# Attention's gathering of v: v as the stationary operand, both halves of a block in two column tiles, turned back per block

## The chip, the core and the metric

The kernel runs on one core of a Trainium2 chip. The metric is the device time of one execution, in microseconds (us); lower is better. The chip's engines run side by side, each with its own instruction stream in a fixed order: TensorE (PE, with its weight loads shown apart as PEld), VectorE (DVE), ScalarE (ACT), GpSimd (POOL) and SyncE (SP), which issues the transfers.

## What is computed

The program applies four layers to x, of shape 32 x 192 x 56 x 56 in float32, each as x + layer(group norm of x). The change is in layer 0, an attention through 49 "agent" tokens in six heads. Its reference, cut to what matters:

```python
qkv = xf @ Wqkv + bqkv
q, k, v = (qkv[..., :c], qkv[..., c:2 * c], qkv[..., 2 * c:])
agent = qi.mean(axis=(2, 4)).reshape(b, A, c)
...
agent_attn = softmax(einsum('bhad,bhnd->bhan', ah * scale, kh) + pos_bias, axis=-1)
agent_v = einsum('bhan,bhnd->bhad', agent_attn, vh)
...
q_attn = softmax(einsum('bhnd,bhad->bhna', qh * scale, ah) + agent_bias, axis=-1)
out = einsum('bhna,bhad->bhnd', q_attn, agent_v)
...
out = out + dw.transpose(0, 2, 3, 1).reshape(b, n, c)
out = out @ proj_w + proj_b
```

`agent_v` is the product in question: for each head the 49 agents' weights over all 3136 pixels, times v. `dw` is a 3 x 3 depthwise convolution of v.

## The kernel before

Attention is the function `attention` (from L321). It runs over NB = 32 images, called batches here. An image is cut into NK = 4 blocks of columns, three of 16 and one of 8 columns (WIDTHS), and each block into an upper and a lower half of 28 rows: 448 (or 224) pixels per half. A half is further cut into pieces of SUB = 112 pixels, `ns` = 4 (or 2) per half. The six heads are taken as three pairs; one pair has PAIR = 98 agents, and HA = 294 is all of them.

For each block j a first loop does, in this order of the program:

- `weigh` (L592): for each head pair the scores of 98 agents over the block's pixels, on PE (L600, L601); their maximum on DVE (L602, `low`); the exponential on ACT (L604), which leaves `pr` and its sums.
- `seen` for q in block 0, and from block 1 on `gather` of the block before (L633).
- `turn` (L610): the transposes of v (L619, copied by ACT into `vT`, L620) and of `pr` (L627, copied by ACT into `prT`, L630).
- `find_v` (L553) of block j + 2: v on PE, copied by ACT into the padded images `v_a`, `v_c` (L561, L569) and into `v`.
- `convolve` (L575) of block j + 1: eight taps each for two channel groups on DVE (L587). A block's taps read one column of the next block, so they wait for its `find_v`. In the last block `moments` of the next image (L450) takes that place.

`gather` multiplies, for each head pair, `prT` (112 pixels x 98 agents, stationary) by `vT` (112 pixels x 64 channels, streaming) and sums over all pieces of both halves in PSUM; the result has the agents on its partitions, and DVE copies it to `got[:, j]` (L642).

After the loop come `ask(0)` (L666: scores of the pixels over the agents on PE, L674 and L675, their softmax on DVE and ACT, L678 to L691), the last block's `gather`, and `join` (L644), which scales the four blocks' `got` to a common maximum on DVE (L647 to L662) and leaves `values`. A second loop over t then runs `ask(t)`, `turn_back` (L694, transposes L701), `project` (L722) and `answer` (L709, which multiplies `values` by the turned weights, L714 and L719), with the next image's normalisation, agents and first two `find_v` between.

PSUM has four buffers of two banks for all of this (tag "ps"), each given to the next user once its readers are done. A planner orders the instructions on each engine when the program is built; the order is then fixed. On DVE and ACT it differs from the program's in places, for instance one `vT` copy stands before the third exponential. An instruction that waits holds up all that follows on its engine.

Of the kernel before, what the change touches and what calls it, by code (L numbers as in the profile page):

```python
# [20 lines left out]
F32 = mybir.dt.float32  # L21
I32 = mybir.dt.int32
AF = mybir.ActivationFunctionType
ALU = mybir.AluOpType
# [4 lines left out]
C = 192  # L29
# [14 lines left out]
PAIR = 2 * AG  # L44
HA = HEADS * AG
# [275 lines left out]
def attention(ctx: ExitStack, tc: tile.TileContext, a, k, x1):  # L321
# [6 lines left out]
    nc = tc.nc  # L328
# [3 lines left out]
    wp = ctx.enter_context(tc.tile_pool(name="a_w", bufs=2))  # L332
    sp = ctx.enter_context(tc.tile_pool(name="a_s", bufs=2))
    pp = ctx.enter_context(tc.tile_pool(name="a_p", bufs=4, space=PSUM))
    mm = nc.tensor.matmul
    UP, LOW = slice(0, 64), slice(64, 128)
    HALVES = ((0, UP), (1, LOW))
    P2 = slice(0, PAIR)

    def psum():  # L340
        return pp.tile([128, 2, BANK], F32, name="ps", tag="ps")
# [85 lines left out]
    def small(name, shape):  # L427
        return sp.tile(shape, F32, name=name, tag=name)
# [21 lines left out]
    def moments(x):  # L450

        st_a, st_c = small("st_a", [128, 7, 6]), small("st_c", [128, 4, 6])
        flat = [t.rearrange("p y x -> p (y x)") for t in x]
        for i in range(7):
            nc.vector.bn_stats(st_a[:, i], flat[0][:, i * 448 : (i + 1) * 448])
        for i in range(4):
            nc.vector.bn_stats(st_c[:, i], flat[1][:, i * 392 : (i + 1) * 392])
        mv = small("mv", [128, 2, 2])
        nc.vector.bn_aggr(mv[:, 0], st_a.rearrange("p a b -> p (a b)"))
        nc.vector.bn_aggr(mv[:, 1], st_c.rearrange("p a b -> p (a b)"))  # L460
        pool_a, pool_c = small("pool_a", [128, AG]), small("pool_c", [65, AG])
        by_x = [wp.tile([128, n, POOL], F32, name="by_x", tag=f"by_x{n}", bufs=1) for n in (S, S // 2)]
        for t in range(2):
            nc.vector.tensor_reduce(
                by_x[t].rearrange("p y q -> p (y q)"), x[t].rearrange("p y (q x) -> p (y q) x", x=8), AX.X, ALU.add
            )
        nc.vector.tensor_reduce(
            pool_a.rearrange("p (w q) -> p w q", w=POOL), by_x[0].rearrange("p (w y) q -> p w q y", y=8), AX.X, ALU.add
        )
        fours = small("fours", [64, 2 * POOL, POOL])  # L470
        for h, r in HALVES:
            nc.vector.tensor_reduce(
                fours[:, h * POOL : (h + 1) * POOL], by_x[1][r].rearrange("p (w y) q -> p w q y", y=4), AX.X, ALU.add
            )
        nc.vector.tensor_tensor(
            pool_c[0:64].rearrange("p (w q) -> p w q", w=POOL), fours[:, 0::2], fours[:, 1::2], ALU.add
        )
        nc.vector.memset(pool_c[64:65], 1.0)
        return mv, (pool_a, pool_c)
# [130 lines left out]
    def turn(j, prs, v):  # L610

        _, _, ns = sizes(j)
        vT = wp.tile([SUB, 4, 3 * 128], F32, name="vT", tag="vT")
        for s0 in range(0, ns, 2):
            ps = psum()
            for i in range(2):
                px = slice((s0 + i) * SUB, (s0 + i + 1) * SUB)
                for c in range(3):
                    nc.tensor.transpose(ps[:SUB, i, c * 128 : (c + 1) * 128], v[:, c, px], ident)  # L619
            nc.scalar.copy(vT[:, s0 : s0 + 2], ps[:SUB, :, : 3 * 128])  # L620
        prT = wp.tile([SUB, 8, HA], F32, name="prT", tag="turned", bufs=2)
        for q in range(0, 2 * ns, 2):
            ps = psum()
            for i in range(2):
                h, s = divmod(q + i, ns)
                for p in range(3):
                    nc.tensor.transpose(  # L627
                        ps[:SUB, i, p * PAIR : (p + 1) * PAIR], prs[p][:, h, s * SUB : (s + 1) * SUB], ident[P2, P2]
                    )
            nc.scalar.copy(prT[:, q : q + 2], ps[:SUB, :, :HA])  # L630
        return prT, vT

    def gather(j, prT, vT, got):  # L633
        _, _, ns = sizes(j)
        ps = psum()
        for p in range(3):
            out = ps[P2, 0, p * 64 : (p + 1) * 64]
            for q in range(2 * ns):
                h, s = divmod(q, ns)
                c = h * 128 + p * 64 if p < 2 else 256 + h * 64  # L640
                mm(out, prT[:, q, p * PAIR : (p + 1) * PAIR], vT[:, s, c : c + 64], start=(q == 0), stop=(q == 2 * ns - 1))
        nc.vector.tensor_copy(got[:, j], ps[P2, 0, :C])  # L642

    def join(low, sums, got):  # L644

# [20 lines left out]
    def ask(j, g):  # L666
        _, _, ns = sizes(j)
        pq = wp.tile([SUB, 8, HA], F32, name="pq", tag="turned", bufs=2)
        for q0 in range(0, 2 * ns, 4):
            for q in range(q0, q0 + 4, 2):  # L670
                ps = psum()
                for i in range(2):
                    px = slice((q + i) * SUB, (q + i + 1) * SUB)
                    mm(ps[:SUB, i, :HA], xs_a[j][:, px], g, start=True, stop=False)  # L674
                    mm(ps[:SUB, i, :HA], xs_c[j][0:KC, px], gq_c[0:KC, 2 * j + (q + i) // ns], start=False, stop=True)  # L675
                by_head = ps[:SUB, :, :HA].rearrange("p i (h g) -> p i h g", g=AG)
                mx = sp.tile([SUB, 2, HEADS], F32, name="mx", tag="mx", bufs=4)
                nc.vector.tensor_reduce(mx, by_head, AX.X, ALU.max)  # L678
                nc.vector.tensor_tensor(
                    pq[:, q : q + 2].rearrange("p i (h g) -> p i h g", g=AG),  # L680
                    by_head,
                    _bc(mx, [SUB, 2, HEADS, AG]),
                    ALU.subtract,
                )
            flat = pq[:, q0 : q0 + 4].rearrange("p i c -> p (i c)")
            rows = flat.rearrange("p (r g) -> p r g", g=AG)
            nc.scalar.activation(flat, flat, AF.Exp)
            sm = sp.tile([SUB, 4 * HEADS], F32, name="sm", tag="sm", bufs=4)
            nc.vector.tensor_reduce(sm, rows, AX.X, ALU.add)
            nc.vector.reciprocal(sm, sm)  # L690
            nc.vector.tensor_tensor(rows, rows, _bc(sm, [SUB, 4 * HEADS, AG]), ALU.mult)  # L691
        return pq
# [53 lines left out]
    for b in range(NB):  # L746
        x, more = nxt, b + 1 < NB
        if more:
            nxt = load(b + 1)
        low, sums, got = small("low", [PAIR, NK, 3]), small("sums", [PAIR, NK, 3]), small("got", [PAIR, NK, C])  # L750
        turned, asked, back = {}, {}, {}
        for j in range(NK):
            prs = weigh(j, gk, low, sums)
            if j == 0:
                gq = seen(ag, wqT, gq_c, "gq_a")
            else:
                gather(j - 1, *turned[j - 1], got)
            turned[j] = turn(j, prs, v[j])
            if j + 2 < NK:
                v[j + 2] = find_v(j + 2)  # L760
            if j + 1 < NK:
                o[j + 1] = convolve(j + 1)
            elif more:
                mv, pools = moments(nxt)
        asked[0] = ask(0, gq)
        gather(NK - 1, *turned[NK - 1], got)
        values = join(low, sums, got)
        done, o = o, {}
        for t in range(1, NK + 2):
            if t < NK:  # L770
                asked[t] = ask(t, gq)
            if more and t == 1:
                mean, d = spread_of(mv)
            if t <= NK:
                back[t - 1] = turn_back(t - 1, asked[t - 1])
            if more and t in (3, 4):
                v[t - 3] = find_v(t - 3)
            if t >= 2:
                project(t - 2, done[t - 2], x)
            if t <= NK:  # L780
                answer(t - 1, back[t - 1], values, done[t - 1])
            if more and t == 1:
                rs, nb = scaling(mean, d, pools)
                normed(nxt, rs, nb, 0)
            if more and t == 2:
                ag = find_agents(b + 1, pools)
                normed(nxt, rs, nb, 1)
            if more and t == 3:
                gk = seen(ag, wkT, gk_c, "gk_a")
                normed(nxt, rs, nb, 2)  # L790
            if more and t == 4:
                o[0] = convolve(0)
                normed(nxt, rs, nb, 3)
        nc.sync.dma_start(out=x1[b, 0:128], in_=x[0].rearrange("p y x -> p (y x)"))
        for h, r in HALVES:
            nc.sync.dma_start(out=x1[b, 128:C, 1568 * h : 1568 * h + 1568], in_=x[1][r].rearrange("p y x -> p (y x)"))
# [909 lines left out]
```

## Time and profile before

| what | value |
|---|---|
| median of 3 runs | 14596.81 us (14577.73 to 14602.56) |
| profiled execution, its own time | 14588.21 us |
| profiled execution, span of its instructions | 14586.4 us |
| granted TensorE clock, mean | 0.927 |
| busy: PE, PEld, DVE, ACT, POOL | 84%, 52%, 78%, 41%, 15% |
| attention loop | about 330 to 5320 us |
| in it busy: PE, DVE, ACT | 4662, 4022 and 2369 of 4990 us |
| gather's matmuls (L641) | 5376 matmul records (as many weight loads), median 250 ns (167 ns) |
| gather's copy (L642) | 128 on DVE, median 356 ns |

Busy time is the time in which an engine has an instruction in flight, as a share of the span. Matmuls are pipelined and overlap each other in the records, so the spacing of their starts says more than the length of one. A float32 matmul of the program shows as two records of PE and two weight loads, a transpose as one. Idle time stands before the instruction that ended it, with the engine and line that released it. "granted clock" is the share of full speed that TensorE's clock was given.

### The profile page before, as it was taken

To read this page: it belongs to the slowest core of one execution; us is meant where nothing else is said; L and a number is where in the kernel's file an instruction comes from. 1 tells how busy PE (TensorE), PEld (TensorE's weight loads), DVE (VectorE), ACT (ScalarE), POOL (GpSimd) and SP (SyncE) were. 2 spreads that over 40 slices of the span, in tenths; PEclk is the share of its full clock that TensorE was granted. 3 is DMA by queue.
4 is the path that set the end of the run, shared out by engine and by line. 5 is a ranking of instruction groups with operands and counts; after the bars stand their busy time and mean duration, and the time that the engine had idled before them with its cause. 6 is when DMAs were issued, how large, how long until landed. Compare 5 with 4: busy or idle time off the path is not lost. (4 is left out here: it accounts for less than half of the span.)

```text
span 14586.4 us, 164705 instructions
## 1 busy us (share of the span) xinstructions
PE 12276.2 (84%) x63542; PEld 7620.1 (52%) x63542; DVE 11320.3 (78%) x15929; ACT 5972.2 (41%) x10826; POOL 2178.7 (15%) x2238
## 2 busy tenths in 40 slices
PE   4999999999999976777677677767899889988898
PEld 2655655655565553333333333335666666666666
DVE  4878877887887878878887887886777777777777
ACT  2444444444444434444444444443323232323323
POOL 0000000000000004434443443442000000000000
PEclk8999999999999988888888888888999999999999
DMA  2001001000100112232223222322111111111111
GB/s 54 27 27 40 27 27 40 27 27 32 35 27 27 40 53 66 60 71 71 65 67 81 66 60 68 75 51 56 35 37 36 37 37 36 37 35 38 36 37 23
DMA packets 886784, 654.14 MB, mean 45 GB/s; under 512 B 764942, under 2 KB 772857, under 8 KB 876976
## 3 DMA queue, kind: packets, MB, share of 16 engines
q1 hardware_dynamic: 885992, 643.51, 16.7%
q8 instruction: 505, 8.27, 0.2%
q14 instruction: 287, 2.35, 0.1%
HBM read 402.88 MB, written 240.50 MB: 44 GB/s over the span
## 5 line engine op out<-in xcount | busy, mean ns | idle before, releaser
L587 DVE SCALAR_TENSOR_TENSOR o<-v_a,dww,o 128x896 f32<-128x896 f32 (+1 forms) x1024 | 1052.8, 1028 | 390.1 <-ACT v_a L561 282.7
L1633 ACT COPY y<-ps 64x252 f32<-64x252 f32 (+1 forms) x2376 | 807.6, 340 | 1298.6 <-PE ps L1627 1266.4
L1567 PE MATMUL ps<-f,imag 84*84 84x112 f32 x6144 | 1032.0, 261 | 130.2 <-DVE imag L1560 128.5
L1574 ACT COPY z<-ps 84x448 f32<-84x448 f32 x768 | 405.3, 528 | 1771.1 <-PE ps L1567 1771.1
L1567 PE MATMUL ps<-f,real 84*84 84x112 f32 x6144 | 1035.7, 261 | 1.7
L1567 PEld LDWEIGHTS ps<-f,imag 84*84 84x84 f32 x6144 | 744.0, 153 | 275.6 <-DVE imag L1560 206.4
L1567 PEld LDWEIGHTS ps<-f,real 84*84 84x84 f32 x6144 | 748.8, 153 | 160.1 <-issue 68.6
L1041 ACT ACTIVATE q<-q 128x784 f32<-128x784 f32 x384 | 329.3, 858 | 1225.4 <-DVE q L1036 1223.9
L1035 POOL COPY c<-p 128x1 f32<-128x1 f32 x384 | 696.2, 1813 | 665.3 <-DVE p L1034 611.8
L1048 POOL MEMSET c<- 128x1 f32 x192 | 18.3, 99 | 5182.8 <-PE ps L719 5172.1
L1034 DVE TENSOR_TENSOR_SCAN q<-decay,c,ek 128x784 f32<-128x784 f32 x384 | 702.0, 1832 | 105.3 <-ACT ek L1064 105.2
L1583 PE MATMUL ps<-z,f 84*114 84x448 f32 x1536 | 658.5, 551 | 129.5 <-ACT z L1574 129.5
L604 ACT ACTIVATE pr<-ps,low 98x896 f32<-98x896 f32 (+1 forms) x384 | 350.1, 914 | 1015.4 <-DVE low L602 1015.4
L1585 DVE TENSOR_TENSOR o<-ps,rs 114x448 f32<-114x448 f32 x384 | 239.5, 624 | 631.7 <-PE ps L1583 630.5
L1035 POOL COPY c<-q 128x1 f32<-128x1 f32 x384 | 483.1, 1258 | 1460.7 <-DVE q L1034 1390.3
L1034 DVE TENSOR_TENSOR_SCAN p<-decay,c,bv 128x784 f32<-128x784 f32 x384 | 699.9, 1833 | 0.0
L674 PE MATMUL ps<-gq_a,xs_a 128*112 128x294 f32 x1792 | 643.7, 442 | 0.0
L600 PE MATMUL ps<-xs_a,gk_a 128*98 128x448 f32 (+1 forms) x1536 | 639.0, 497 | 0.0
L587 DVE SCALAR_TENSOR_TENSOR o<-v_c,dww,o 128x448 f32<-128x448 f32 (+1 forms) x1024 | 634.0, 619 | 4.0
L1547 PE MATMUL re<-y,f 128*84 128x420 f32 (+1 forms) x1152 | 561.5, 569 | 84.8 <-ACT y L1633 74.8
L601 PE MATMUL ps<-xs_c,gk_c 125*98 125x448 f32 (+1 forms) x1536 | 631.6, 492 | 0.0
L675 PE MATMUL ps<-gq_c,xs_c 125*112 125x294 f32 x1792 | 627.7, 433 | 0.0
(352 smaller groups left out, 29243.6 us busy)
## 6 DMA issues: line engine op xcount, KB each, us to landing
x<-x SPq DMA_DIRECT2D x512, 392.0 KB
x<-x SPq DMA_DIRECT2D x512, 196.0 KB
x<-x SPq DMA_DIRECT2D x192, 399.0 KB
out_x<-x SPq DMA_DIRECT2D x384, 196.0 KB
x_a<-in_x SPq DMA_DIRECT2D x32, 1568.0 KB
x<-x_a SPq DMA_DIRECT2D x32, 1568.0 KB
x_c<-in_x SPq DMA_DIRECT2D x64, 392.0 KB
x<-x_c SPq DMA_DIRECT2D x64, 392.0 KB
```

The costliest lines, as they stand in the source:

```text
L587: nc.vector.scalar_tensor_tensor(dst, tap(i), dww[:, t, i : i + 1], dst, ALU.mult, ALU.add)
L600: mm(ps[P2, h, :n], g[:, cols], xs_a[j][:, px], start=True, stop=False)
L601: mm(ps[P2, h, :n], gk_c[0:KC, 2 * j + h, cols], xs_c[j][0:KC, px], start=False, stop=True)
L674: mm(ps[:SUB, i, :HA], xs_a[j][:, px], g, start=True, stop=False)
L675: mm(ps[:SUB, i, :HA], xs_c[j][0:KC, px], gq_c[0:KC, 2 * j + (q + i) // ns], start=False, stop=True)
L1034: nc.vector.tensor_tensor_scan(out, decay[:, of(t)].to_broadcast([128, MC]), data, at, ALU.mult, ALU.add)
L1035: nc.gpsimd.tensor_copy(at, s[:, last : last + 1])
L1547: nc.tensor.matmul(ps[:, : n * 84], f2[:, i, :], y[:, i0 : i0 + n].rearrange("p g s u -> p (g s u)"), start=True, stop=True)
L1567: nc.tensor.matmul(ps[:84, i * 2 * S : (i + 1) * 2 * S], part[:, i0 + i].rearrange("p s u -> p (s u)"), f3[:, m, :], start=(m == 0), stop= ...
L1574: nc.scalar.copy(z[:, i0 : i0 + n].rearrange("p g m w -> p (g m w)"), ps[:84, : n * 2 * S])
L1583: nc.tensor.matmul(got, f4[:, m, :], z[:, i0 : i0 + n, m, :], start=(m == 0), stop=(m == 1))
L1633: nc.scalar.copy(y[64 * m : 64 * m + 64, 2 * g0 + i : 2 * (g0 + n) : 2], got[64 * i : 64 * i + 64, :, :, m, :])
```

## The change

`gather` exchanges the operands: `vT` (64 channels of one half) is stationary, `prT` (98 agents) streams. The upper half's products go to PSUM partitions 0 to 63 and the lower half's to 64 to 127, so that neighbouring matmuls of the two halves lie in two column tiles of the array. The sum then has channels on the partitions and the halves apart. ACT copies it to a new tile `halves`. A new function `settle` turns it back with three transposes, after which ACT copies one half to `got` and DVE adds the other. `settle` stands behind `turn` of the following block. The last block's `gather` moves from behind `ask(0)` to in front of it, and its `settle` stands behind `ask(0)`. `got` has one buffer instead of two.

```diff
-    def gather(j, prT, vT, got):
+    def gather(j, prT, vT):
+
         _, _, ns = sizes(j)
         ps = psum()
         for p in range(3):
-            out = ps[P2, 0, p * 64 : (p + 1) * 64]
-            for q in range(2 * ns):
-                h, s = divmod(q, ns)
-                c = h * 128 + p * 64 if p < 2 else 256 + h * 64
-                mm(out, prT[:, q, p * PAIR : (p + 1) * PAIR], vT[:, s, c : c + 64], start=(q == 0), stop=(q == 2 * ns - 1))
-        nc.vector.tensor_copy(got[:, j], ps[P2, 0, :C])
+            cols = slice(p * PAIR, (p + 1) * PAIR)
+            for s in range(ns):
+                for h, r in HALVES:
+                    c = h * 128 + p * 64 if p < 2 else 256 + h * 64
+                    mm(ps[r, 0, cols], vT[:, s, c : c + 64], prT[:, h * ns + s, cols], start=(s == 0), stop=(s == ns - 1))
+        halves = wp.tile([128, HA], F32, name="halves", tag="halves")
+        nc.scalar.copy(halves, ps[:, 0, :HA])
+        return halves
+
+    def settle(j, halves, got):
+
+        ps = psum()
+        for p in range(3):
+            nc.tensor.transpose(ps[P2, 0, p * 128 : (p + 1) * 128], halves[:, p * PAIR : (p + 1) * PAIR], ident)
+        both = ps[P2, 0, : 3 * 128].rearrange("p (a h d) -> p a h d", a=3, h=2)
+        nc.scalar.copy(got[:, j].rearrange("p (a d) -> p a d", a=3), both[:, :, 0])
+        mine = got[:, j].rearrange("p (a d) -> p a d", a=3)
+        nc.vector.tensor_tensor(mine, mine, both[:, :, 1], ALU.add)
...
-        low, sums, got = small("low", [PAIR, NK, 3]), small("sums", [PAIR, NK, 3]), small("got", [PAIR, NK, C])
+        low, sums = small("low", [PAIR, NK, 3]), small("sums", [PAIR, NK, 3])
+        got = sp.tile([PAIR, NK, C], F32, name="got", tag="got", bufs=1)
         turned, asked, back = {}, {}, {}
         for j in range(NK):
             prs = weigh(j, gk, low, sums)
             if j == 0:
                 gq = seen(ag, wqT, gq_c, "gq_a")
             else:
-                gather(j - 1, *turned[j - 1], got)
+                halves = gather(j - 1, *turned[j - 1])
             turned[j] = turn(j, prs, v[j])
+            if j > 0:
+                settle(j - 1, halves, got)
             if j + 2 < NK:
                 v[j + 2] = find_v(j + 2)
...
+        halves = gather(NK - 1, *turned[NK - 1])
         asked[0] = ask(0, gq)
-        gather(NK - 1, *turned[NK - 1], got)
+        settle(NK - 1, halves, got)
         values = join(low, sums, got)
```

## The prediction

> **What bounds the kernel now.** The change touches the attention stage alone, so I first look for that stage and for its limit. The page's busy shares in 40 slices (one slice is 365 us) show it: PE at nine tenths from slice 2 on, DVE at seven or eight.
>
> ```profile
> PE   4999999999999976777677677767899889988898
> ...
> DVE  4878877887887878878887887886777777777777
> ...
> PEclk8999999999999988888888888888999999999999
> ```
>
> The whole attention loop runs from about 330 to 5320 us, 32 batches of 158.7 us (by the starts of gq_a's copy, L533: 157.7 and 159.7 in turn). Read as one stage it says "PE". I cut one batch into three stretches (busy us and counts of PE, PEld, DVE, ACT, POOL, then granted clock):
>
> ```profile
> 2052.60:2122.00 69.40, 66.35 (x408) 44.77 (x406) 59.33 (x85) 33.78 (x62) 0.00 (x0) 1.00 0.22 70
> 2122.00:2150.00 28.00, 25.01 (x134) 17.58 (x132) 27.16 (x45) 8.53 (x10) 0.00 (x0) 0.96 0.00 1
> ```
>
> Where three of the four gathers stand (first row) PE is busy 66.4 of 69.4 us. Where ask, join and the first answer stand (second row) DVE is: 27.2 of 28.0. So time saved on PE ahead of that stretch counts only if DVE's chain moves too. Next, the timeline of PE, ACT and DVE around the first gather (start, us, what, idle before):
>
> ```profile
> 2082.81 4.29 PE L641 MATMUL ps<-vT,prT 112*98 112x64 f32 x48
> 2086.94 1.48 PE L619 MATMUL ps<-ident,v 128*112 128x128 f32 x12
> 2088.25 0.78 PE L627 MATMUL ps<-ident,pr 98*112 98x98 f32 x4
> 2089.65 1.90 PE L627 MATMUL ps<-ident,pr 98*112 98x98 f32 x20 [0.62 <-ACT pr L604]
> 2091.38 0.57 PE L559 MATMUL ps<-xs_a,wv_a 128*128 128x224 f32 x2
> ```
> ```profile
> 2087.80 0.80 ACT L620 COPY vT<-ps 112x768 f32<-112x768 f32 x1 [0.96 <-PE ps L619]
> 2088.49 1.01 ACT L604 ACTIVATE pr<-ps,low 98x896 f32<-98x896 f32 x1
> ```
> ```profile
> 2084.62 2.08 DVE L602 TENSOR_REDUCE low<-ps 98x1 f32<-98x896 f32 x2
> 2087.14 0.36 DVE L642 COPY got<-ps 98x192 f32<-98x192 f32 x1 [0.44 <-PE ps L641]
> ```
>
> The turning of pr (L627) waits for the third exponential, which ends at 2089.5. DVE has its maximum by 2086.7, behind eight pairs of convolution taps; between, ACT's fixed order puts a vT copy that waits for PE. So the gather stands beside the chain find_v, convolve (DVE), maxima, exponentials, turn, find_v; it is not the chain.
>
> **The gather itself.** Before: 24 matmuls, two records each, 48 x 86 ns = 4.13 us (2082.81 to 2086.94): 64 columns stream, but a weight load of 98 columns goes with each. Half block: 24 records, 2.04 us. After: weights of 64 columns, 98 columns streaming, neighbours in two column tiles. No row shows this shape; the nearest pair of column tiles is answer:
>
> ```profile
> 2047.62 0.93 PE L714 MATMUL ps<-pqT,values 98*64 98x224 f32 x8
> 2048.38 0.55 PE L719 MATMUL ps<-pqT,values 98*64 98x224 f32 x4
> ```
>
> Eight records of 224 columns start within 0.76 us: 190 ns for a pair, what one alone takes at full width (L600 with 224 columns: 0.38 us for two). So two run side by side. For 98 columns L627 gives 1.73 us / 20 = 86 ns, so 24 pairs take 2.06 us. Going into column tiles and out costs 0.09 us each and a slower first record 0.05 (L566, which starts at 2093.02 after 2092.55 + 0.38, and L600 after it). Value taken: 2.3 us; half block 1.3. Bounds: 2.1, and 4.4 if the pairs don't overlap at this size.
>
> **What is added on PE.** Three transposes of 128 columns per block, 12 L619 in 1.31 us: 0.33. PE alone thus saves 3 x (4.13 - 2.3 - 0.33) + (2.04 - 1.3 - 0.33) = 4.9 us a batch, 157 us in all. That is what a PE bound would give.
>
> **On ACT:** halves, 128x294, as gq_a (L533), 0.41 us; the copy of 98x192, near v_c's 128x224 (0.38): 0.3. Together 2.8 us a batch; ACT is busy 34 of 69 us, but halves stands in front of the third exponential. **On DVE:** the copy of 0.36 goes, an add of the same size (L662: 0.29) comes: nothing, bounds -0.1 and +0.1 each. Its wait is new: transposes and ACT's copy come first, in ACT's order behind four prT copies. The adds have 0.3 us to spare in block 1 and over 1.5 later. No DMA is added; got in one buffer is first written some 40 us after join has read it. A fifth psum user per block is released by the add; the four buffers hold it as long as the add isn't queued behind the taps.
>
> **The path, block by block.** Block 1: gather ends 1.85 us earlier, the vT copy can follow the second exponential at 2086.84 instead of waiting to 2087.80, the third exponential comes 0.94 earlier (halves fits before the second), L627 too; settle gives 0.33 back: -0.6. DVE's next taps wait for v_a, so they follow by 0.6 (DVE itself is ready 0.9 earlier). Block 2: third exponential -1.05, settle +0.33: -0.72, not the sum, since the maxima moved by only 0.6. Block 3's weigh, 4.57 us, is PE work; gather(2) there gives its full 1.85: -2.57 at the end of turn(3), 2119.45. Now the step that moves: gather(3) stands before ask(0) instead of after it, and needs turn(3)'s two prT copies:
>
> ```profile
> 2121.17 0.80 ACT L620 COPY vT<-ps 112x768 f32<-112x768 f32 x1 [3.25 <-PE ps L619]
> 2121.87 1.20 ACT L630 COPY prT<-ps 112x588 f32<-112x588 f32 x2
> ```
>
> They end at 2123.07, 1.05 us after the last L627. ask(0) was the cover. Settle(2) fills 0.33; 0.7 of wait and 1.3 of gather are left. ask(0) starts at -2.57 + 0.33 + 0.7 + 1.3 = -0.2 us. After it only settle(3) stands, so ask(1) is 1.9 us early, but DVE is not:
>
> ```profile
> 2128.28 0.77 DVE L678 TENSOR_REDUCE mx<-ps 112x12 f32<-112x588 f32 x1 [0.79 <-PE ps L675]
> ...
> 2145.69 0.29 DVE L662 TENSOR_TENSOR values<-values,heads 98x192 f32<-98x192 f32 x1
> ```
>
> From ask(0)'s third pair to values it has no idle time of note, and answer(0) already waits 1.73 us for values. So values comes 0.2 us earlier: -0.2 x 32 = -6 us.
>
> **What the idle time does.** The saved time becomes PE idle: about 1.9 us before L627 in blocks 1 and 2 (0.9 now), and 2.0 before turn_back(0) (0.37 now). Two stretches of 3.4 us at the same place (turn(0)) of two batches:
>
> ```profile
> 2062.33:2065.74 3.41, 2.51 (x18) 1.77 (x17) 0.68 (x1) 2.31 (x2) 0.00 (x0) 1.00 0.90 309
> ...
> 2222.60:2226.00 3.40, 1.77 (x18) 1.56 (x19) 0.00 (x0) 3.40 (x6) 0.00 (x0) 1.00 1.00 301
> 2226.00:2229.50 3.50, 3.50 (x13) 2.27 (x11) 1.68 (x3) 2.13 (x4) 0.00 (x0) 0.52 0.52 149
> ```
>
> After a stretch with PE busy 1.77 us the granted clock halves for the next; after 2.51 it does not. Its price: from turn(0)'s resumption to turn(1)'s 22.75 us in the first batch (2066.90 to 2089.65), 24.37 in the second (2224.61 to 2248.98): 1.6 us. With 1.9 us idle, a stretch that holds most of it is busy about 1.5 us, less than 1.77. How the stretches fall decides, so each of the two places is hit about six times in ten: 1.3 us at block 1 (0.3 of it covered by DVE), 1.6 at block 2, and 0.9 at turn_back(0) (half of its transposes at half speed). Bounds: 0 and 3.8 us a batch. I take one halving more per batch, 1.6. Sum: (-0.2 + 1.6) x 32 = +45 us on the profiled execution's 14588.2 (span 14586.4): 14633. The median of the runs shown lies 9 us higher; I leave that in the range.
>
> The Trainium skill ("TensorE: Matmul & The Clock Gate", on the clock gate and its oscillation) speaks of the clock falling after an idle window of about 3.4 us and advises against gaps over that. By it stalls of 1.9 us would cost nothing and the sum would be 14582; the rows above show a halving after a window more than half busy, and I go by them. Its "TensorEngine Tiling" page (PSUM bottleneck) warns that tiling speeds up TensorE but not the emptying of PSUM; here the emptying is doubled in number, at the 2.8 us of ACT counted above.
>
> **Rivals.** (1) The lead gets through: ask(0)'s matmuls fill the wait for prT, or maxima are ordered earlier. DVE's waits of 0.44, 0.42, 0.38 and 0.79 us vanish: 2.0 x 32 = 65, 14523; if PE were the only bound, 14431. For it: PE's 66.4 of 69.4. Against it: DVE's 27.2 of 28.0, and PE keeps the order of the program in every row I read. 25%. (2) The same chain, no halving more: 14582, no change. 20%. (3) The column pairs don't overlap with weights so short-lived: each gather costs 4.4 + 0.33, three blocks 1.8 us, gather(3) in front of ask(0) 2.3 + 0.7: 4.7 x 32 = 150, 14738. It decides once a pair takes over 130 ns. Against it: L714. 10%. The forecast, with 14595 to 14703 as its own range, has 45%.
>
> **Numbers.** About 0.2% (29 us) can be told from no change. Faster: 24 from (1), 2 from (2): 0.26. Same (14568 to 14626, the median +- 29): 9 from the forecast, 15 and 1: 0.25. Slower: 0.49. The range 14510 to 14710 leaves out the depth of (1) and (3).
>
> **What would show it.** L641's 48 records starting within 2.1 to 2.4 us; L627 waiting 1.5 us or more for pr; ask(0) starting no earlier in the batch; answer(0) waiting over 3 us for values; more stretches at half clock in slices 2 to 14. It is wrong if PE's idle time per batch stays near 10 us, or if gather(3) stands behind ask(0)'s first pairs.

## The result, and the profile after

| | before | after |
|---|---|---|
| median of 22 runs each | 14594.83 us (14573 to 14606) | 14560.76 us (14535 to 14651) |
| ratio after to before, 95% | | 0.9996 [0.9979, 1.0012] |
| profiled execution, own time (span) | 14588.21 (14586.4) | 14537.30 (14535.5) |
| attention loop of that execution ends at | 5362 us | 5331 us |
| length of a batch in it | 157.7 and 159.7 in turn | 157.0, every seventh 160.2 |
| PE idle in a batch | 10.1 to 10.9 us | 13.2 us |
| PE at half clock between 400 and 5200 us of it | 314 us | 365 us |

No change that can be measured. The ratio weighs all runs; the two medians alone lie 0.23% apart, because that of the changed kernel falls into the lower of two groups. One thing has to be known to read the numbers: the runs of the changed kernel fall in two groups, 13 between 14535 and 14575 us and 9 between 14637 and 14651, while those of the kernel before form one. The profiled execution is of the lower group; one of the upper group comes among the experiments. Of the 51 us between the two profiled executions 31 lie in the attention loop. The rest lies behind it, where the code is the same: that part took 9200 to 9235 us in the twelve profiles of this study, in no order that follows an edit, so those 20 us are put down to nothing.

The busy shares in 40 slices of the changed kernel, to be held against the three rows of before:

```profile
PE   4999999999999976777677677767888989888888
...
DVE  4878888887888868878887887886777777777777
...
PEclk8999999999999988888888888888999999999999
```

Nothing is to be seen at this grain: in attention (slices 1 to 14) PE's row is the same, and DVE's differs by a tenth here and there. The two stretches of a batch that the prediction cut, at the same places of the same batch, do show something (stretch; us; busy us and count of PE, PEld, DVE, ACT, POOL; granted clock):

```profile
2042.83:2112.23 69.40, 65.06 (x445) 40.92 (x444) 60.69 (x86) 36.69 (x70) 0.00 (x0) 1.00 0.22 70
2112.23:2140.23 28.00, 23.90 (x109) 16.69 (x107) 25.62 (x43) 8.02 (x10) 0.00 (x0) 0.88 0.00 1
```

In the stretch of the gathers PE is 1.3 us less busy. In the stretch of ask, join and the first answer DVE, which had 0.8 us to spare, now has 2.4, and the granted clock fell from 0.96 to 0.88. A lead came in, and DVE stands idle at the end of it. Before, PE had this in the same place (start, us, what, idle before):

```profile
2141.42 1.71 PE L701 MATMUL ps<-ident,pq 112*98 112x112 f32 x16 [0.37 <-DVE f L655]
2143.42 0.97 PE L701 MATMUL ps<-ident,pq 112*98 112x112 f32 x8 [0.29 <-ACT pqT L705]
2146.13 1.78 PE L714 MATMUL ps<-pqT,values 98*64 98x448 f32 x8 [1.73 <-DVE values L662]
```

The 24 transposes of turn_back(0) (here L701) run at full clock, and answer(0) (here L714) waits for values. The timeline of PE after (start, us, what, idle before):

```profile
2109.65 0.38 PE L642 MATMUL ps<-prT,vT 112*64 112x98 f32 x2
2109.97 0.75 PE L687 MATMUL ps<-gq_a,xs_a 128*112 128x294 f32 x2
2110.64 1.22 PE L642 MATMUL ps<-prT,vT 112*64 112x98 f32 x22
...
2128.72 1.02 PE L485 MATMUL ps<-mv,norm 128*128 128x1 f32 x8 [0.94 <-DVE pq L692]
2131.72 1.70 PE L714 MATMUL ps<-ident,pq 112*98 112x112 f32 x8 [1.98 <-DVE pq L692]
2134.41 3.22 PE L714 MATMUL ps<-ident,pq 112*98 112x112 f32 x16 [0.99 <-ACT pqT L718]
2137.57 1.72 PE L727 MATMUL ps<-pqT,values 98*64 98x448 f32 x8
```

ask(0) (L687) starts in the middle of gather(3) (L642), not behind it. Later PE waits 0.94 and 1.98 us, and the transposes of turn_back(0) (now L714), 8 of which took 0.97 us before, take 1.70 us for 8 and 3.22 for 16. DVE in that place, before and then after:

```profile
2140.54 0.74 DVE L679 TENSOR_TENSOR pq<-ps,mx 112x588 f32<-112x588 f32 x1
...
2141.95 0.94 DVE L657 TENSOR_TENSOR got<-got,f 98x768 f32<-98x768 f32 x1
...
2144.11 1.45 DVE L661 TENSOR_REDUCE values<-got 98x192 f32<-98x768 f32 x1
```
```profile
2126.94 0.95 DVE L670 TENSOR_TENSOR got<-got,f 98x768 f32<-98x768 f32 x1
...
2128.49 1.46 DVE L674 TENSOR_REDUCE values<-got 98x192 f32<-98x768 f32 x1
...
2130.54 0.35 DVE L675 TENSOR_TENSOR values<-values,heads 98x192 f32<-98x192 f32 x1
2130.81 0.76 DVE L692 TENSOR_TENSOR pq<-ps,mx 112x588 f32<-112x588 f32 x1
...
2139.34 1.09 DVE L729 TENSOR_TENSOR o<-o,ps 128x896 f32<-128x896 f32 x1 [2.02 <-PE ps L727]
```

values is there at 2130.9, 6.7 us before answer(0) (L727) starts: it is not what answer waits for any more. The two long steps of join (L657 and L661 before, L670 and L674 after) stood behind the second subtraction of ask(1) (L679 before, L692 after) and stand in front of it now. The same stretch in the windows of the granted clock (columns as above):

```profile
2127.28:2130.70 3.42, 1.52 (x11) 0.99 (x9) 3.42 (x5) 0.00 (x0) 0.00 (x0) 1.00 0.00 0
2130.70:2134.10 3.40, 1.70 (x8) 1.36 (x8) 3.40 (x5) 1.83 (x2) 0.00 (x0) 0.50 0.01 2
2134.10:2137.50 3.40, 3.09 (x16) 2.85 (x16) 3.19 (x7) 1.17 (x2) 0.00 (x0) 0.50 0.00 0
2137.50:2140.95 3.45, 2.54 (x13) 0.77 (x12) 1.61 (x2) 1.99 (x2) 0.00 (x0) 1.00 0.00 0
2140.95:2144.36 3.41, 1.67 (x11) 1.52 (x12) 3.04 (x7) 0.28 (x2) 0.00 (x0) 1.00 0.02 5
2144.36:2147.77 3.41, 3.41 (x8) 2.16 (x7) 1.41 (x5) 3.15 (x5) 0.00 (x0) 0.50 0.00 0
```

A window with PE busy 1.52 us is followed by one at half clock; that one, at half clock and waiting, is busy 1.70 and followed by another; and so again at 2140.95.

All this against the kernel before, as offsets from the start of gq_a's copy (L533) in one batch (before 2063.43 us, one of its batches of 157.7 us; after 2053.66, one of 157.0). In before's other batches, of 159.7 us, the clock halves once at the start, and all rows from ask(0) to answer(0) stand 1.6 us later:

| us from the start of the batch | before | after | difference |
|---|---|---|---|
| rest of turn(1) resumes (L627) | 26.22 | 25.16 | -1.06 |
| find_v(3) | 27.95 | 27.22 | -0.73 |
| weigh(3) | 48.19 | 46.78 | -1.41 |
| ask(0), first matmul | 58.60 | 56.30 | -2.30 |
| DVE's third maximum of ask(0) | 64.85 | 63.91 | -0.94 |
| values complete | 82.56 | 77.23 | -5.33 |
| turn_back(0), first transpose | 77.99 | 78.05 | +0.06 |
| turn_back(0), last transpose ends | 80.97 | 83.97 | +3.00 |
| answer(0) | 82.70 | 83.90 | +1.20 |
| group sum of d (L485) | 88.40 | 89.03 | +0.63 |
| ask(2) | 90.13 | 89.91 | -0.22 |

A lead of 5.3 us at values is a lead of 0.2 us at ask(2). Two things stand between: turn_back(0) cannot start earlier, and then it runs at half speed.

### The profile page after: what moved, and what is told of

Same layout as the page of the kernel before. It is cut to its first block, busy times and chain, and to the rows that moved or that the text cites. A ratio compares the mean times of both kernels' runs of the same rounds, so it can differ in the third digit from the quotient of the medians.

```text
span 14535.5 us, 165764 instructions
## 1 busy us (share of the span) xinstructions
PE 12136.9 (83%) x63926; PEld 7408.2 (51%) x63926; DVE 11323.8 (78%) x15929; ACT 6043.4 (42%) x11082; POOL 2198.0 (15%) x2238
## 5 line engine op out<-in xcount | busy, mean ns | idle before, releaser
L687 PE MATMUL ps<-gq_a,xs_a 128*112 128x294 f32 x1792 | 632.7, 435 | 0.0
```

## The experiments

Three theories stand against each other: that the move of gather(3) in front of ask(0) gives back what the gather's form saves; that the lost clock does, turn_back(0) being the place; and that the gather's work was never on the path, so that neither its form nor its size matters. For each kernel the median, and the ratio to the runs of before taken on the same chip.

**The form without the move.** After, with gather(3) back behind ask(0):

```diff
-        halves = gather(NK - 1, *turned[NK - 1])
         asked[0] = ask(0, gq)
+        halves = gather(NK - 1, *turned[NK - 1])
         settle(NK - 1, halves, got)
```

> The changed kernel with the last block's gather put back behind ask(0), its settle right after it; the rest as changed. Theory A (what decides is the stretch from ask(0) to answer(0): there the planner's order on DVE and the clock, not the gather's length): join's steps go back between ask(1)'s on DVE, values ends about 82 us after the copy of gq_a instead of 77; ask(0) starts 1 to 2 us earlier; turn_back(0) waits less for PSUM. The time moves by more than 20 us against the changed kernel's 14537 to 14575 or 14638 to 14651, to either side. Theory B (the shorter gathers give the gain, the place of the last one gives nothing): within 15 us of the changed kernel's faster runs, 14535 to 14560.

Measured: 14585.37 us, 0.9992 [0.9983, 1.0], some 40 us above the median of the changed kernel's lower group, as theory A had it; but values came at 78.9 and not at 82. ask(0) comes 2.89 us earlier than before, 0.6 more than in the changed kernel; values at 78.88, turn_back(0) starts at 76.68, 1.31 earlier than before, and answer(0) at 81.89 instead of 82.70. Yet ask(2) is at 90.49, 0.36 later than before, and between 400 and 5200 us the loop spends 519 us at half clock instead of 314. In a batch that starts at 2064.44, turn_back(0) reads:

```profile
2141.12 1.53 PE L714 MATMUL ps<-ident,pq 112*98 112x112 f32 x8 [1.92 <-DVE pq L692]
2143.20 3.20 PE L714 MATMUL ps<-ident,pq 112*98 112x112 f32 x16 [0.56 <-DVE pq L692]
```

The same wait for L692 and the same half speed without the move. The move costs 1.4 us at the start of turn_back(0), but the rest of the lead is lost without it too.

**The move without the form.** Before, with only the last gather in front of ask(0):

```diff
+        gather(NK - 1, *turned[NK - 1], got)
         asked[0] = ask(0, gq)
-        gather(NK - 1, *turned[NK - 1], got)
         values = join(low, sums, got)
```

> The kernel of before with one edit, the last block's gather in front of ask(0). Theory A: on DVE join's steps move ahead of ask(1)'s as in the changed kernel, values ends 3 to 5 us earlier in the batch, but ask(0) starts 2 to 3 us later (gather 2.04 us and a wait of 1 us for prT in front of it); ask(2) starts 0 to 3 us later, 14590 to 14690. Theory B: the place gives nothing, 14575 to 14605 as before.

Measured: 14679.22 us, 1.0058 [1.0046, 1.007]; ask(0) 0.94 later, DVE's third maximum 2.64 later, answer(0) 4.30 later. Alone the move costs 0.58%, some 85 us or 2.6 a batch. PE around it, in a batch that starts at 2094.07:

```profile
2153.22 0.56 PE L641 MATMUL ps<-vT,prT 112*98 112x64 f32 x4 [0.42 <-ACT prT L630]
2153.61 0.70 PE L674 MATMUL ps<-gq_a,xs_a 128*112 128x294 f32 x2
2154.15 1.87 PE L641 MATMUL ps<-vT,prT 112*98 112x64 f32 x20
```

Here too the first half of ask(0)'s first pair (L674) slips in, next to a wait for a copy of prT of 0.42 us; but the rest of the gather, 20 records in 1.7 us, stays in front of the second half, and so of DVE's first maximum. The planner also puts join's small steps before ask(1)'s in this kernel, as in the changed one: values is complete at 81.27, 1.3 earlier than before although everything around is 2.6 later. So the early join comes from the move: in both kernels that have it join's two long steps stand in front of ask(1)'s second subtraction; before both stand behind it, and in the form without the move one does.

**Filling the first idle stretch.** After, with two matmuls of 512 columns in the unused second PSUM bank of the first group sum (the batch's `mv`); nobody reads them:

```diff
+    def fill(ps, n):
+        for _ in range(n):
+            mm(ps[:, 1, :512], ident, norm4.rearrange("p a b -> p (a b)"), start=True, stop=True)
...
-                mean, d = spread_of(mv)
+                mean, d = spread_of(mv, 2)
```

> The changed kernel with two matmuls of 512 columns added after the batch's first group sums (on the second, unused bank of that PSUM tile; 1.7 us of PE, which waits there for 2.0 us). It computes the same. Theory A: PE's clock does not halve before turn_back(0), whose 24 transposes take 2.3 us of PE instead of 4.3; answer(0) starts about 1 us earlier, 20 to 40 us less than the changed kernel, and the runs of 14640 to 14650 get rarer. Theory C (the clock there is covered by DVE's own chain): no change against the changed kernel, or up to 10 us more.

Measured: 14550.55 us, 0.9968 [0.9956, 0.998], all six runs within 14540 to 14569. The timeline of PE, in a batch that starts at 2057.57, and its windows:

```profile
2133.49 1.96 PE L483 MATMUL ps<-norm,ident 128*128 128x512 f32 x4
2135.60 0.95 PE L719 MATMUL ps<-ident,pq 112*98 112x112 f32 x8 [0.15 <-DVE pq L697]
2137.58 0.97 PE L719 MATMUL ps<-ident,pq 112*98 112x112 f32 x8 [1.03 <-ACT pqT L723]
2138.88 0.97 PE L719 MATMUL ps<-ident,pq 112*98 112x112 f32 x8 [0.32 <-DVE pq L697]
```
```profile
2137.00:2144.80 7.80, 4.35 (x28) 2.27 (x28) 7.39 (x14) 3.42 (x4) 0.00 (x0) 1.00 0.00 0
2144.80:2151.60 6.80, 6.69 (x18) 4.95 (x19) 2.98 (x7) 4.34 (x7) 0.00 (x0) 0.51 0.00 0
```

The filling (L483) fills the wait for L692, turn_back (here L719) keeps the full clock at the same start, answer(0) comes 1.68 us earlier than in the changed kernel. The batch still has 157.0 us: PE is idle again behind answer(0), and the clock halves there, for two windows, under ask(2). What one place gained the next took: the upper group of runs is gone, but against the lower one (14535 to 14575) this is no gain.

**Filling both.** The same and two more behind answer(0):

> As the run before it, and two more such matmuls behind answer(0), where PE waits 2.65 us for DVE. Theory A: ask(2) runs at full clock from its start, 1.7 us per batch less than with the first filling alone, some 50 us: 14440 to 14500. Theory C: PE is early there anyway, within 15 us of the run with the first filling alone.

Measured: 14471.32 us, 0.9911 [0.9898, 0.9923]. Of the 365 us at half clock between 400 and 5200 us 45 are left, mostly single windows at the start of a batch (columns as for the windows above; the clock is rounded):

```profile
400.00:5200.00 4800.00, 4482.05 (x25238) 2680.03 (x25237) 3958.82 (x5655) 2401.05 (x4001) 0.00 (x0) 1.00 0.10 31
```

**Before, with both fillings.** Does the gather's form matter once the clock holds?

> The kernel of before with the same two fillings (two matmuls after the first group sums, two after answer(0)). Theory D (the clock was the loss in both kernels, the gather's form brings little): it falls about as far as the changed kernel did with them, to 14480 to 14520. Theory E (the shorter gathers count once the clock holds): the clock holds here too, but the time stays above 14530, some 60 us or more above the changed kernel with both fillings (14471).

Measured: 14480.70 us, 0.9917 [0.9904, 0.993]. The fillings alone give the old kernel as much; 48 us at half clock are left of 314:

```profile
400.00:5200.00 4800.00, 4577.97 (x24822) 2882.32 (x24822) 3953.84 (x5644) 2332.29 (x3750) 0.00 (x0) 1.00 0.10 31
```

With the same clock PE is 96 us less busy in the changed kernel of these two (4482 against 4578 us) and DVE the same within 5 us; the times cannot be told apart, with intervals of some 19 us to either side, and the two profiled loops end 10 us apart. The saving on PE is real, and it does not set the end.

**The form without the move, filled.**

> The changed kernel with the last gather back behind ask(0) and both fillings. If the move gives what the changed kernel has (join's steps early on DVE), this stands above 14471 by about as much as values ends later, 1 to 1.7 us per batch, 14500 to 14530. If the move gives nothing once the clock holds: 14460 to 14490.

Measured: 14544.70 us, 0.9963 [0.995, 0.9976]. Neither expected range was met, and this one settled nothing by itself, for 225 us at half clock were left: in each batch one or two windows at offsets 87 to 91. With four fillings behind answer(0) instead of two:

> The changed kernel with the last gather behind ask(0) and the first filling, and four matmuls instead of two behind answer(0), since two left PE idle for 2.3 us there and the clock still halved at 87 us of each batch. If the place of the last gather gives nothing once the clock holds: no stretch at half clock left in the loop, batches of 154 to 155 us, 14460 to 14490 as the two filled kernels. If the move itself gives time: batches of 156 us or more at full clock, above 14500.

Measured: 14467.27 us, 0.9916 [0.9903, 0.993], with 38 us at half clock left. So with the clock held three kernels cannot be told apart: old form 0.9917, new form with the move 0.9911, new form without it 0.9916. The move costs nothing that shows in the new form, and the new form brings nothing that shows; what a bound by PE would have brought was 157 us. It also answers a rival, that the fillings help through another order of the planner: in the changed kernel and in the one before, the filling behind answer(0) does change the order on DVE and ACT. Here it does not. This kernel and the same without fillings (14585 us) have one order of instructions on PE, DVE and ACT in the batches compared, the filling matmuls aside; what differs is 38 us at half clock for 519, and 118 us of time.

**The filling behind answer(0) alone.**

> The changed kernel with the filling behind answer(0) alone. If the clock's fall before turn_back(0) costs only where DVE is late anyway, it stands near the kernel with both fillings, 14470 to 14500. If answer(0)'s delay by it (1.7 us) goes to the end, 14515 to 14540, and the two groups of runs stay away or come back, which this run is to show.

Measured: 14543.31 us, 0.9966 [0.9955, 0.9977], 3 us above the second of the expected ranges. turn_back(0) is at half clock as in the changed kernel; the place at 91 keeps its clock, while in two batches of three one window at the start (offset 4) loses it. answer(0) is at 85.45 in such a batch and at 83.60 in one without it. Either filling alone brings 0.3%, both 0.9%: one halving that is left, or comes elsewhere, takes most of what the other filling brought.

**Gathers nearly free.** Both fillings, and each gather multiplies only the first piece of each half, so that the rest of the keys is left out of the sum:

```diff
-            for s in range(ns):
+            for s in range(1):
...
-                    mm(ps[r, 0, cols], vT[:, s, c : c + 64], prT[:, h * ns + s, cols], start=(s == 0), stop=(s == ns - 1))
+                    mm(ps[r, 0, cols], vT[:, s, c : c + 64], prT[:, h * ns + s, cols], start=True, stop=True)
```

> The changed kernel with both fillings, and in gather only the first of a half's four (or two) pieces is multiplied; the other pieces are left out of the sum. PE loses 1.6 us of matmuls in each of three gathers and 0.5 in the last. Theory A (the gathers stand beside the chain of DVE and ACT): less than 0.8 us per batch, 14445 to 14475. Theory B (gathers count fully): 5.3 us per batch, about 14300.

Measured: 14512.33 us, 0.9944 [0.9932, 0.9957], against 0.9911 [0.9898, 0.9923] with the whole gather: 41 us *slower* by the medians, and above both expected ranges. The windows at turn(1) and turn(2), in a batch that starts at 2035.8:

```profile
2058.20:2061.60 3.40, 1.85 (x16) 1.23 (x15) 3.40 (x4) 2.78 (x6) 0.00 (x0) 1.00 0.00 0
2061.60:2065.00 3.40, 3.40 (x20) 3.30 (x19) 2.79 (x7) 2.71 (x5) 0.00 (x0) 0.53 0.02 5
...
2078.70:2082.10 3.40, 1.50 (x11) 1.08 (x11) 3.40 (x7) 3.40 (x8) 0.00 (x0) 1.00 0.00 0
2082.10:2085.50 3.40, 3.40 (x22) 3.39 (x23) 3.40 (x7) 2.60 (x5) 0.00 (x0) 0.53 0.00 0
```

These rows lie 0.2 us off the windows in which the clock is granted; on them PE is busy 1.87 and 1.67 us. Less work on PE here left two windows with PE busy under 1.9 us, and the clock halved behind each; 305 us at half clock stand in the loop against 45. The planner's order on DVE differs too in this kernel (values at 83.4), so the 41 us are not all shown to be the clock's. What it does show is that this smaller gather did not shorten the batch; what it would bring at full clock stays open.

**The changed kernel once more**, unchanged:

> The changed kernel once more, unchanged. Its runs fell into two groups, 14535 to 14575 and 14638 to 14651. Theory A (batches lock to the steps in which the clock is granted): a profile in the upper group shows batches of about 160.3 us with one long stretch at half clock, one in the lower group batches of 157.0 us. Otherwise, if the groups come from elsewhere, the attention loop is equally long in both.

Measured: 14552.60 us, 0.9996 [0.9976, 1.0016]: seven runs at 14540 to 14553, five at 14637 to 14661; its profiled execution (14637.18) is of the upper group. There all batches have 160.4 us, and the clock halves at the start of the batch as well (the batch starts at 2092.48):

```profile
2097.50:2100.90 3.40, 3.40 (x11) 2.08 (x10) 1.54 (x3) 1.96 (x4) 0.00 (x0) 0.51 0.49 151
...
2169.20:2172.60 3.40, 1.43 (x13) 1.37 (x14) 3.40 (x6) 0.52 (x1) 0.00 (x0) 1.00 0.01 2
2172.60:2176.05 3.45, 2.45 (x15) 2.08 (x13) 3.45 (x6) 1.57 (x2) 0.00 (x0) 0.51 0.00 0
2176.05:2179.45 3.40, 3.40 (x15) 1.92 (x15) 1.66 (x4) 2.75 (x3) 0.00 (x0) 0.50 0.00 0
```

509 us at half clock between 400 and 5200 us against 365; attention ends at 5427 us instead of 5331, and these 96 us are about the distance of the two groups. Where the windows fall in the batch is what differs. 157.0 us are 46 windows of 3.413 us, 160.4 are 47, seven batches of the lower group's profile (six of 157.0, one of 160.2) are 323, and before's pair of 157.7 and 159.7 is 93: the batch falls in step with the windows and keeps the place where it fell. So the sum of half clock alone does not give the time: the form without the move has 519 us of it, before 314, and both take 93 windows for two batches. How a loop comes into step, and whether a run's first batches decide which of the two it is, was not tried. With the first place filled or the second only one group is left, of 6 and of 7 runs.

## Why the prediction was right and wrong

The forecast was 14633 us, slower, likeliest; measured was no change, 72 us below it and inside the range. The upper group of runs (14637 to 14651) is where the forecast stood, the lower lies 0.1 to 0.4% below the median of before. That the upper group meets the forecast is in good part luck, as the steps below show; no change is what rival (2) gave, but with the old chain and the old clock, and neither was kept.

*The gather's cost* was right. 48 records in 2.24 us where 2.3 were taken, and settle in 0.33:

```profile
2073.14 2.24 PE L642 MATMUL ps<-prT,vT 112*64 112x98 f32 x48
2075.53 1.52 PE L619 MATMUL ps<-ident,v 128*112 128x128 f32 x12 [0.15 <-ACT pr L604]
2077.13 0.38 PE L627 MATMUL ps<-ident,pr 98*112 98x98 f32 x2
2077.82 0.38 PE L627 MATMUL ps<-ident,pr 98*112 98x98 f32 x2 [0.31 <-ACT vT L620]
2078.82 1.90 PE L627 MATMUL ps<-ident,pr 98*112 98x98 f32 x20 [0.62 <-ACT pr L604]
2080.55 0.49 PE L651 MATMUL ps<-ident,halves 128*98 128x128 f32 x3
```

Rival (3), pairs that don't overlap, is out. *ACT and DVE*: ACT's two copies 0.40 and 0.36 us (0.41 and 0.3 taken), DVE's add 0.345; as predicted.

*The stage's bound* was right, and it is the point that held best: the times of the three filled kernels (old form, new form with and without the move) cannot be told apart, though PE's busy time differs by 96 us between the first two. Rival (1)'s deep end, 14431, with PE as the only bound, is out. With the clock held a batch has 154 to 156 us in the old and the new form; which chain sets these was not settled beyond "not the gather".

*Blocks 1 and 2* were nearly right: L627 1.06 earlier for 0.94, find_v 0.73 for 0.6. Block 2 gained 1.41 for 0.72, because in it the planner now has the third exponential ahead of vT's copy.

*The halvings at turn(1) and turn(2)* did not come. The stalls are 1.08 us in block 1 (0.15, 0.31, 0.62 above) and 1.40 in block 2 (0.81 and 0.59), not 1.9 each: the saved time went partly into an earlier start. The windows that hold them keep the clock:

```profile
2076.08:2079.49 3.41, 2.41 (x21) 1.78 (x20) 3.41 (x4) 3.41 (x7) 0.00 (x0) 1.00 0.00 0
...
2093.14:2096.56 3.42, 2.61 (x50) 2.42 (x47) 3.42 (x5) 2.04 (x4) 0.00 (x0) 1.00 0.00 0
2096.56:2099.97 3.41, 2.82 (x31) 2.55 (x30) 3.41 (x8) 3.41 (x8) 0.00 (x0) 1.00 0.00 0
```

The rule behind the step, that a window with PE about half busy halves the next, stood: with less gather left both places halve. Its own row of 1.77 us lies 0.16 us off the window in which the clock is granted, and in that window PE is busy 1.94. The size of the stall was wrong.

*The halving at turn_back(0)* came in every batch looked at and was undersized: two windows, not one, +1.7 us at the end of turn_back (82.28 with the first place filled against 83.97) where 0.9 was taken. The half clock under ask(2), at offset 91, is not new: before's batches have it at 90 to 97 or, in the others, at 84 to 94.

*"values -0.2"* failed, and with it "PE keeps the order of the program". The planner put ask(0)'s first matmul into the wait of gather(3), and on DVE it moved join's steps ahead of ask(1)'s, as it does for the move alone. That is the condition of rival (1), but its 14523 us did not come. values came 5.33 us earlier. The step assumed that values was what answer(0) waits for; it was, before, but 1.7 us behind stood turn_back(0), which needs a PSUM buffer that ask(1)'s subtraction on DVE (L692) gives free. That subtraction ended at 77.85 before and at 77.91 after, and turn_back(0) started 0.14 us behind it in both, as it did in the kernels with the form or the move alone; the row of before names L655, the small step of join beside it. It did not move although DVE's third maximum was 0.94 earlier: join's two long steps, 2.4 us, now stand in front of it, while shorter ones went. In the form without the move one of the two stands there, and it ends at 76.53. That is the wait that took the place of the one removed: predicted was that answer(0) would wait over 3 us for values, and it waits for turn_back.

*"one halving more per batch"* is the step on which the sum fell. PE's idle time went from 10.5 to 13.2 us a batch, which is more, as forecast. But half clock rose by 51 us in some 30 batches (314 to 365), half a window a batch where one was taken, and the mean batch fell from 158.7 to 157.6 us where 1.4 more was forecast. Most batches of the lower group's profile have 6.83 + 3.41 = 10.24 us at half clock, and before's have 10.24 too (10.24 in one piece, or 3.41 at turn(0) and 6.83 under ask(2)): two windows at turn_back(0) came, others went; every seventh batch has 20.48. The upper group's profile has 3.41 + 6.83 + 6.83 = 17.07, two windows more, and ends attention 65 us later than before. Its batch of 160.4 us is 1.8 longer, near the 1.4 of the forecast, but not by the forecast's places: nothing halves at turn(1) and turn(2), and two windows at turn_back(0) and one at the start of every batch, before of every second, do. What the step left out is that a loop can fall in step with the windows, and that it then decides which places are hit.

The Trainium skill ("TensorE: Matmul & The Clock Gate", section "HAM oscillation — how this bites in real kernels") gives as its abstract rule that PE have no idle gaps over about 3.4 us. No gap in the changed kernel's batches between the first and the last is over 2.66 us; it lost the clock after windows that held two or three shorter gaps and were busy 1.4 to 1.7 us in sum. The measurement decides: the busy time of a window counts, not the longest gap.

## What to carry to other kernels

Before work is taken off an engine that looks full, look at which engine has no idle time in the stretch behind it and at which buffer it must give free: what was won stops there (a lead of 5.3 us at values, of 0.2 at ask(2)). On PE the saved time can cost more than nothing, for it turns into idle time, and idle time in the wrong window into half a clock. Where windows of 3.4 us with PE less than about half busy stand in a loop, a few matmuls that nobody reads are worth a try: some 2 us of them at each of two places of a 158 us batch gave 0.9% here, where the change gave nothing, and the kernel before with them is as fast as any version that was run.

## What was not expected of the hardware

- Half-clock stretches in the loop are multiples of 3.41 us, and their windows stand on one grid in each profile. Over the twelve profiles, from 420 to 5190 us, all 379 full-clock windows with PE busy under 1.74 us were followed by half clock, 172 of the 320 between 1.74 and 2.10, and one of the 15148 above. The same page of the skill (section "What's actually happening") has free-running windows of 3.413 us, which agrees.
- A loop whose length depends on where the windows fall can settle on a whole number of them. One program then has two times, 0.7% apart, on the same chip. A median over 22 runs of it is a mixture, and a profile shows one of the two.
- A stretch already at half clock prolongs itself more easily: it is busy 1.70 us of 3.40 with waits in it (2130.70 above), and the next one is halved too. So were all 261 half-clock windows of the twelve profiles with PE busy under 3.0 us, and still 109 of the 664 above.
